# A decoder layer with routed experts: two ticks of attention scores joined into one round

## The chip, the core and the metric

The kernel runs on one core of one Trainium2 chip. The metric is the device time of one execution in microseconds. A run takes the whole layer: self-attention, cross-attention and a feed-forward part with 64 routed experts and a shared expert, all in fp32, for 32 sequences of 256 tokens and width 256.

## The reference

Cut to what matters here (16 heads, head width 16, T = 256 tokens, S = 120 context tokens):

```python
# self-attention, per sequence
q, k, v = heads(x @ qkv_w + qkv_b);  q, k = rotary(q), rotary(k)
x = layernorm(x + (softmax(q @ k.T * 16**-0.5) @ v) @ out_w + out_b)
# differential cross-attention: two half-heads of width 8
q1, q2 = halves(x @ qw.T + qb);  k1, k2 = halves(ctx @ kw.T + kb);  v = ctx @ vw.T + vb
a = softmax(q1 @ k1.T * 8**-0.5) - lam * softmax(q2 @ k2.T * 8**-0.5)
x = layernorm(x + ((a @ v) * (1 - LAMBDA_INIT)) @ out_proj.T + b)
# feed-forward: 6 of 64 experts per token, at most 96 rows per expert, and a shared expert
scores = sigmoid(x @ router.T); top 6; xs[slot] = x[token]
y = gelu(xs @ w1) @ w2;  out[token] += weight * y
x = layernorm(out + gelu(x @ sw1.T) @ sw2.T)
```

The routing goes over all 8192 tokens in order; a token that finds an expert's 96 rows taken gets nothing from it.

## The kernel before, in words

One stage makes both attentions and the routing for all 32 sequences ("batches" in the code); a second stage runs the experts in pairs, adds the shared expert's result and normalises. The change is in the first stage.

**Order.** Every engine is wrapped by `InOrder` (lines 166 to 192). It ties each instruction to the one before it on the same engine, so that each engine works in exactly the order in which the program writes the calls. All these calls are recorded with the wrapper's line 175; groups in the profile are therefore told apart by their tiles and not by their lines. Semaphores between engines come from the tiles: a buffer is written again when its last reader is done.

**Ticks.** `class Batch` writes its steps into the dictionary `plan`, keyed by tick and part. For each tick the loop at line 1015 runs "pre", then the score products, then their readers, then "av", "mm" and "post". "pre" mostly empties the PSUM banks that the tick before has filled; "mm" holds TensorE's other pieces: projections, transposes, the routing's products. A batch's self part starts at `start` and its cross part at `cross`. In the middle of the stage a new batch starts each 16 ticks, with its cross part 72 ticks after its self part. The first five self parts and the last four cross parts stand 8 ticks apart.

**Scores.** The softmax needs each row's maximum. So the scores are made twice. `maxima(k)` makes the scores of two heads with queries on the partitions, and VectorE reduces them (`pad_mx<-sc`). `turn_max` transposes the maxima, ScalarE copies them (`mT`), and GpSimd adds them into the queries' spare rows (`add_max`, `qT<-qT,mT`). Ten ticks after the maxima `weights(k)` makes the scores again, with keys on the partitions, and ScalarE takes the exponential (`pt<-sc`). A head uses 32 rows of the array. A tick has two heads' maxima on two strips of 32 rows and two heads' weights on the other two, so that four matmuls run side by side:

```python
for n in range(2):
    for mms, _ in pairs:
        for dst, lhsT, rhs in mms[2 * n : 2 * n + 2]:
            pe.matmul(dst, lhsT=lhsT, rhs=rhs, start=True, stop=True)
for _, read in pairs:
    read()
```

Each of these matmuls is two in the profile, as every fp32 matmul is; a tick's scores are 16 records. In the profile `sc<-qT,kT` are the weights and `sc<-kT,qT` the maxima.

**PSUM.** Of the eight banks, the pool `scp` has four, as two tiles of two banks (`sc`), and the pool `trp` four single banks (`tr`, `av`). A tick's two score tiles take both of `scp`; all other pieces share `trp`.

**Other pieces.** `values` and `xvalues` multiply the exponentials by the values (`av<-pt,pad_v`, 32-column strips); `back` and `xback` transpose the results, `weigh` and `xweigh` divide by the softmax's sums. `project_qk` and `rotate` make queries and keys, with the rotation on GpSimd (VectorE for the first batch). `heads` transposes them into `kT` and `qT`. `residual_1`, `residual_2`, `stats` and `normalise` close each attention; the routing follows (`router`, `route`, `places`, `keys`, `slots_of`). `dispatch` then scatters token rows into `slots` by indirect DMAs from GpSimd, twelve for a batch. The shared expert (`shared`) is a generator. Its pieces (tile `h` and others) are drawn one at a time near the stage's end and in the second stage.

Of the kernel before, what the change touches and what calls it, by code (L numbers as in the profile page):

```python
# [19 lines left out]
P = 128  # L20
# [17 lines left out]
def tile_decoder_layer(  # L38
# [74 lines left out]
    w_s1 = weights(sw1T, "w_s1")  # L113
    w_s2 = weights(sw2T, "w_s2")
# [81 lines left out]
    scp = ctx.enter_context(tc.tile_pool(name="scp", bufs=2, space=PSUM))  # L196
    trp = ctx.enter_context(tc.tile_pool(name="trp", bufs=4, space=PSUM))

    def bank():
        return trp.tile([P, 512], F32, tag="tr", name="tr")  # L200
# [4 lines left out]
    ys, whole = {}, set()  # L205

    def shared(ypool):
# [23 lines left out]
        before = None  # L231
        loaded = {k: load(k) for k in range(3)}
        gTs = {}
        for k in range(NBLK + 1):
            for f2 in range(2):
# [4 lines left out]
                if before:  # L240
                    before()
                hp = scp.tile([P, 2, 512], F32, tag="sc", name="h")
# [11 lines left out]
                before = lambda hp=hp, gT=gT: gelu(hp, gT)  # L254
                yield
            for q2 in range(NQ // 2):
                if k == 0:
                    continue
                if before:
                    before()  # L260
                ps = bank().rearrange("p (q d) -> p q d", q=2)
                for q in range(2):
                    for f in range(SF // P):
                        pe.matmul(
                            ps[:, q, :],
                            lhsT=gTs[k - 1, f // 2][
                                :, f % 2, (2 * q2 + q) * P : (2 * q2 + q + 1) * P
                            ],
                            rhs=w_s2[:, f, :],
                            start=(f == 0),  # L270
                            stop=(f == SF // P - 1),
                        )
                before = lambda k=k, q2=q2, ps=ps: keep(k - 1, q2, ps)
                yield
        before()
# [6 lines left out]
    with ExitStack() as one:  # L282
# [5 lines left out]
        small = one.enter_context(tc.tile_pool(name="small", bufs=2))  # L288
        hs = HD // 2
        TICKS = 16  # L290
# [24 lines left out]
        pad_mx = padded([P, NI, 4, PW], "pad_mx", 2)  # L315
# [11 lines left out]
        pad_xv = padded([P, H, PW], "pad_xv", 4, [lambda t: t[:, :, c0]])  # L327
# [51 lines left out]
        plan[-13, "pre"] = [(load_late, ())]  # L379
        for n in range(NE * CAP // (6 * P)):  # L380
            plan[40 + n, "pre"] = [(clear, (n,))]
        plan[5, "mm"] = [(fold, ())]
# [5 lines left out]
        class Batch:  # L388
            taken = None

            def __init__(self, b):
# [9 lines left out]
                turn = B - AHEAD  # L401
                blocks = (
# [3 lines left out]
                self.start, self.cross = (TICKS // 2 * n for n in blocks)  # L406
                self.m1, self.e1, self.m2, self.e2 = (
                    t + k for t in (self.start, self.cross) for k in (0, 10)
                )
                for begin, steps in ((self.start, self.steps()), (self.cross, self.steps_x())):  # L410
                    for tick, part, f, *args in steps:
                        plan.setdefault((begin + tick, part), []).append((f, args))

            def steps(self):


                return [
                    (-15 - (self.start if self.start <= TICKS else 0), "pre", self.load),
                    (-13, "mm", self.project_qk, 0),
                    (-12, "pre", self.rotate, 0),  # L420
                    (-11, "mm", self.project_qk, 1),
                    (-10, "pre", self.rotate, 1),
                    (7, "mm", self.project_v),
                    (8, "pre", self.put_v),
                    (-4, "mm", self.heads, "kT", 0, lambda i: self.qk[:, i, 1]),
                    (-4, "mm", self.heads, "kT", 1, lambda i: self.qk[:, i, 1]),
                    (-3, "pre", self.heads_moved, "kT", 0),
                    (-3, "pre", self.heads_moved, "kT", 1),
                    (-3, "mm", self.heads, "qT", 0, lambda i: self.qk[:, i, 0]),
                    (-2, "pre", self.heads_moved, "qT", 0),  # L430
                    (8, "pre", self.bias_x),
                    (0, "mm", self.heads, "qT", 1, lambda i: self.qk[:, i, 0]),
                    (1, "pre", self.heads_moved, "qT", 1),
                    (8, "mm", self.turn_max, 0),
                    (9, "pre", self.add_max, "qT"),
                    (14, "av", self.values, 0),
                    (14, "av", self.values, 1),
                    (15, "pre", self.values_moved, 0),
                    (18, "av", self.values, 2),
                    (18, "av", self.values, 3),  # L440
                    (19, "pre", self.values_moved, 1),
                    (20, "mm", self.back, 0),
                    (20, "mm", self.back, 1),
                    (21, "pre", self.weigh, 0),
                    (21, "pre", self.weigh, 1),
                    (24, "mm", self.transpose, "aT", lambda: self.at),
                    (25, "pre", self.moved, "aT"),
                    (25, "mm", self.project, "aT", "o", w_out),
                    (26, "pre", self.residual_1),
                    (26, "post", self.stats, 1),  # L450
                    (27, "post", self.normalise, 1),
                    (4 if self.start > TICKS else -14 - self.start, "pre", self.load_x),
                ]

            def steps_x(self):

                out = [
                    (-11, "mm", self.transpose, "x1T", lambda: self.x1),
                    (-9, "pre", self.moved, "x1T"),
                    (-9, "mm", self.project, "x1T", "q", w_xin[:, :, :D]),  # L460
                    (-8, "pre", self.put_q),
                    (2, "post", self.bias_x1),
                    (-8, "mm", self.heads, "yT", 0, lambda i: self.xq[:, i]),
                    (-6, "pre", self.heads_moved, "yT", 0),
                    (-4, "mm", self.heads, "yT", 1, lambda i: self.xq[:, i]),
                    (-3, "pre", self.heads_moved, "yT", 1),
                    (-20, "pre", self.cond_load),
                    (-13, "mm", self.cond_project),
                    (-12, "pre", self.put_kv),
                    (-9, "mm", self.keys_transpose, 0),  # L470
                    (-8, "pre", self.keys_moved, 0),
                    (-7, "mm", self.keys_transpose, 1),
                    (-6, "pre", self.keys_moved, 1),
                    (8, "mm", self.turn_max, 1),
                    (9, "pre", self.add_max, "yT"),
                    (14, "av", self.xvalues, 0),
                    (14, "av", self.xvalues, 1),
                    (15, "pre", self.xvalues_moved, 0),
                    (15, "pre", self.xvalues_moved, 1),
                    (18, "av", self.xvalues, 2),  # L480
                    (18, "av", self.xvalues, 3),
                    (19, "pre", self.xvalues_moved, 2),
                    (19, "pre", self.xvalues_moved, 3),
                    (20, "mm", self.xback, 0),
                    (21, "pre", self.xweigh, 0),
                    (21, "mm", self.xback, 1),
                    (22, "post", self.xweigh, 1),
                    (24, "mm", self.transpose, "bT", lambda: self.at),
                    (25, "pre", self.moved, "bT"),
                    (25, "mm", self.project, "bT", "o", w_xout),  # L490
                    (26, "pre", self.residual_2),
                    (26, "post", self.stats, 2),
                    (27, "post", self.normalise, 2),
                    (28, "mm", self.transpose, "x2T", lambda: self.xpt),
                    (29, "pre", self.moved, "x2T"),
                    (29, "pre", self.store),
                    (32, "mm", self.router),
                    (33, "pre", self.sigmoid),
                    (33, "post", self.route, 0),
                    (35, "post", self.route, 1),  # L500
                    (37, "post", self.route, 2),
                    (39, "post", self.route, 3),
                    (39, "post", self.route, 4),
                    (41, "mm", self.places),
                    (42, "pre", self.keys),
                    (42, "post", self.slots_of),
                ]
                ticks = iter(
                    (43, 43, 45, 47, 50, 51, 51, 52, 52, 53, 55, 55)
# [817 lines left out]
```

## Time and profile before

| | |
|---|---|
| median of 20 runs | 1962.12 us (1951.41 to 1969.15) |
| the profiled execution | 1960.52 us, span 1958.8 us, mean granted TensorE clock 0.982 |
| TensorE busy | 1874.9 us |
| VectorE busy | 1264.1 us |
| ScalarE busy | 1023.3 us |
| GpSimd busy | 1161.8 us |
| last score product | 1587 us after the span's start |
| last scatter of a token row | 1668 us |

The span is the time from the first to the last instruction that the profile records. Busy times of different engines lie beside each other. A matmul's end is modelled, so the start-to-start distances of matmuls say more than their durations.

### The profile page before, as it was taken

To read this page: it belongs to the slowest core of one execution; us is meant where nothing else is said; L and a number is where in the kernel's file an instruction comes from. 1 tells how busy PE (TensorE), PEld (TensorE's weight loads), DVE (VectorE), ACT (ScalarE), POOL (GpSimd) and SP (SyncE) were. 2 spreads that over 40 slices of the span, in tenths; PEclk is the share of its full clock that TensorE was granted. 3 is DMA by queue.
4 is the path that set the end of the run, shared out by engine and by line. 5 is a ranking of instruction groups with operands and counts; after the bars stand their busy time and mean duration, and the time that the engine had idled before them with its cause. 6 is when DMAs were issued, how large, how long until landed. Compare 5 with 4: busy or idle time off the path is not lost.

```text
span 1958.8 us, 43359 instructions
## 1 busy us (share of the span) xinstructions
PE 1874.9 (96%) x17800; PEld 1273.9 (65%) x17800; DVE 1264.1 (65%) x2812; ACT 1023.3 (52%) x1479; POOL 1161.8 (59%) x1155
## 2 busy tenths in 40 slices
PE   7999999999999999999999999999999879898985
PEld 4566666666666666666666666666666656576654
DVE  5456677777777777777777777777767752332175
ACT  1455555555555555555555555555555542321256
POOL 6433456666666666666666666666644567344665
PEclk9999999999999999999999999999999989898998
DMA  4053112111111111111111111111100123786486
GB/s 125 10 129 80 31 48 68 47 43 38 35 37 34 33 35 34 36 34 35 33 31 32 32 32 32 33 32 32 29 24 18 34 77 114 190 230 166 58 316 223
DMA packets 109542, 132.07 MB, mean 67 GB/s; under 512 B 33020, under 2 KB 94677, under 8 KB 109345
## 3 DMA queue, kind: packets, MB, share of 16 engines
q1 hardware_dynamic: 78832, 106.83, 17.6%
q0 software_dynamic: 25600, 13.02, 4.0%
q10 hardware_dynamic: 4912, 9.46, 1.3%
q8 instruction: 140, 2.29, 0.5%
q14 instruction: 58, 0.47, 0.1%
HBM read 74.62 MB, written 111.04 MB: 95 GB/s over the span
## 4 chain that ended last, share of the span: by engine, by line
PE 86%; DMA 6%; DVE 2%; issue 2%; POOL 2%; ACT 2%; ACTq 0%; POOLq 0%; DVEq 0%; SPq 0%
PE tr L175 43%; PE sc L175 28%; PE av L175 12%; DMA acc<-ye,idx 4%; PE h L175 3%; POOL slots L175 1%; DVE pad_mx L175 1%; ACT pt L175 1%; ACT four L175 1%; DMA slots<-xpt,slot 1%; DVE ye L175 0%; DMA xT<-in_xT 0%; DVE xpt L175 0%; DVE st L175 0%; ACT gT L175 0%
## 5 line engine op out<-in xcount | busy, mean ns | idle before, releaser
L175 DVE TENSOR_REDUCE pad_mx<-sc 128x4 f32<-128x1024 f32 (+1 forms) x512 | 609.0, 1190 | 358.7 <-PE sc L175 354.4
L175 ACT ACTIVATE pt<-sc 128x1024 f32<-128x1024 f32 (+1 forms) x512 | 525.0, 1026 | 403.2 <-PE sc L175 401.8
L175 PE MATMUL sc<-qT,kT 32*128 32x256 f32 (+1 forms) x4096 | 578.5, 401 | 8.3 <-ACT pt L175 8.2
L175 PE MATMUL sc<-kT,qT 32*128 32x256 f32 (+1 forms) x4096 | 568.0, 395 | 1.5 <-DVE pad_mx L175 1.5
L175 POOL DMA_INDIRECT slots<-xpt,slot x384 | 390.1, 1016 | 96.0 <-issue 91.4
L175 PEld LDWEIGHTS sc<-qT,kT 32*128 32x128 f32 (+1 forms) x4096 | 343.2, 181 | 131.0 <-issue 63.7
L175 PEld LDWEIGHTS sc<-kT,qT 32*128 32x128 f32 x4096 | 350.6, 185 | 72.4 <-issue 20.9
L175 POOL TENSOR_TENSOR qT<-qT,mT 128x512 f32<-128x512 f32 x128 | 159.6, 1267 | 157.9 <-ACT mT L175 157.9
L175 PE MATMUL tr<-w_qkv,xT 128*128 128x512 f32 (+1 forms) x512 | 194.3, 514 | 8.6 <-DMA xT<-in_xT 8.6
L175 POOL DMA_INDIRECT acc<-ye,idx x64 | 90.5, 1414 | 102.4 <-DVE ye L175 34.3
L175 ACT COPY ot<-av 128x512 f32<-128x512 f32 x192 | 112.6, 586 | 59.6 <-PE av L175 59.3
L175 PEld LDWEIGHTS tr<-w_qkv,xT 128*128 128x128 f32 x512 | 91.1, 192 | 76.6 <-issue 62.4
L175 PE MATMUL h<-x2T,w_s 128*128 128x512 f32 x256 | 123.4, 632 | 16.8 <-ACT gT L175 16.8
L175 POOL TENSOR_SCALAR rs<-mv 128x2 f32<-128x2 f32 x64 | 14.2, 221 | 201.6 <-DVE mv L175 201.5
L175 POOL TENSOR_TENSOR at<-parts 128x256 f32<-128x256 f32 x64 | 46.6, 728 | 141.0 <-DVE parts L175 140.9
L175 PE MATMUL av<-pt,pad_xv 120*32 120x256 f32 x2048 | 124.0, 382 | 0.7 <-ACT ot L175 0.7
L175 PE MATMUL av<-pt,pad_v 128*32 128x256 f32 x2048 | 123.8, 382 | 0.0
L175 PE MATMUL tr<-w_s,gT 128*128 128x256 f32 x512 | 115.9, 384 | 2.3 <-DVE ye L175 2.3
L175 ACT COPY kT<-tr 128x512 f32<-128x512 f32 (+1 forms) x128 | 70.2, 574 | 90.9 <-PE tr L175 90.9
L175 PEld LDWEIGHTS tr<-w_s,gT 128*128 128x128 f32 x512 | 98.0, 192 | 20.6 <-issue 3.8
L175 POOL TENSOR_TENSOR rc<-qkb,cosr 128x512 f32<-128x512 f32 x62 | 80.0, 1290 | 45.3 <-DVE qkb L175 37.3
L175 POOL TENSOR_TENSOR pad_qk<-rc,qkb 128x256 f32<-128x256 f32 x124 | 101.9, 843 | 4.9
(146 smaller groups left out, 2852.5 us busy)
## 6 DMA issues: line engine op xcount, KB each, us to landing
four<-in_w SPq DMA_DIRECT2D x32, 512.0 KB, 4.1
four<-acc SPq DMA_DIRECT2D x32, 512.0 KB, 6.0
xT<-in_xT SPq DMA_DIRECT2D x32, 256.0 KB, 3.4
xt<-in_x SPq DMA_DIRECT2D x32, 256.0 KB, 3.7
x2T_d<-T SPq DMA_DIRECT2D x32, 256.0 KB, 2.4
acc<-xpt SPq DMA_DIRECT2D x32, 256.0 KB, 2.6
acc<-zero SPq DMA_DIRECT2D x32, 256.0 KB
x2T<-x2T_d SPq DMA_DIRECT2D x16, 512.0 KB, 5.5
```

The costliest lines, as they stand in the source:

```text
L175: ins = f(*args, **kwargs)
```

## The change

Two ticks become one round. A round first writes both ticks' score products, four tiles of two banks, which is all of PSUM; then come the four readers, then the other pieces. The pool of the first stage is a ring of four tiles of two banks (`Ring`), from which score tiles and pieces are taken in turn: a piece takes half a tile, and a tile is handed out again when its last reader is done. In the second stage two pools stand apart as before (`Apart`). The weights' tile comes ahead of the maxima's. The table of steps is written anew in rounds; each step has a rank by which the steps of one round and part are sorted, and "av" is merged into "mm". The last batches' cross parts (`tail`) have offsets of their own.

The maxima tile `pad_mx` exists twice for each attention, by the batch's parity. `rotate` is split into `bias_qk` on VectorE, which reads the bank, and the rotation. Buffers: `xT` 3 to 4, `pt` 6 to 8, `xpt` 4 to 3, `pad_xv` 4 to 3. The shared expert's weights `w_s1` and `w_s2` are loaded when its pool opens, 15 rounds after the last batch's self start, and not at the start of the kernel. The arithmetic is unchanged.

```diff
-    scp = ctx.enter_context(tc.tile_pool(name="scp", bufs=2, space=PSUM))
-    trp = ctx.enter_context(tc.tile_pool(name="trp", bufs=4, space=PSUM))
+    class Ring:
+        def __init__(self, stack):
+            self.pool = stack.enter_context(tc.tile_pool(name="ring", bufs=4, space=PSUM))
+            self.half = None
+        def two(self):
+            self.half = None
+            return self.pool.tile([P, 2, 512], F32, tag="two", name="two")
+        def bank(self):
+            if self.half is None:
+                self.half = self.pool.tile([P, 2, 512], F32, tag="two", name="two")
+                return self.half[:, 0, :]
+            t, self.half = self.half, None
+            return t[:, 1, :]
...
-                self.start, self.cross = (TICKS // 2 * n for n in blocks)
+                self.start, self.cross = (4 * n for n in blocks)
...
+                    (-12 - self.start if first else -11, "pre", 0, self.load),
+                    (-10, "mm", 1, self.project_qk, 0),
+                    (-9, "pre", 1, self.bias_qk, 0),
+                    (-9, "post", 3, self.rotate, 0),
+                    (-9, "mm", 0, self.project_qk, 1),
+                    (-8, "pre", 1, self.bias_qk, 1),
+                    (-8, "post", 3, self.rotate, 1),
+                    (-2, "mm", 2, self.heads, "kT", 0, k),
+                    (-2, "mm", 2, self.heads, "qT", 0, q),
+                    (-2, "mm", 2, self.heads, "kT", 1, k),
+                    (-2, "mm", 2, self.heads, "qT", 1, q),
...
+                    (1, "mm", 2, self.project_v),
+                    (4, "mm", 0, self.turn_max, 0),
+                    (4, "post", 0, self.add_max, "qT"),
+                    (8, "mm", 1, self.values, 0),
...
+                    (9, "mm", 0, self.back, 0),
+                    (10, "pre", 0, self.weigh, 0),
+                    (10, "mm", 0, self.transpose, "aT", lambda: self.at),
+                    (11, "mm", 0, self.project, "aT", "o", w_out),
+                    (12, "pre", 0, self.residual_1),
+                    (13, "post", 1, self.stats, 1),
+                    (14, "post", 2, self.normalise, 1),
...
+                    (at(-7, -4), "mm", 2, self.cond_project),
+                    (at(-6, -3), "pre", 2, self.put_kv),
+                    (-5, "mm", 1, self.transpose, "x1T", lambda: self.x1),
+                    (-2, "mm", 1, self.project, "x1T", "q", w_xin[:, :, :D]),
+                    (-2, "mm", 3, self.keys_transpose, 0),
+                    (-1, "pre", 1, self.put_q),
+                    (-1, "mm", 3, self.heads, "yT", 0, lambda i: self.xq[:, i]),
+                    (0, "pre", 2, self.heads_moved, "yT", 0),
+                    (4, "mm", 0, self.turn_max, 1),
+                    (8, "mm", 1, self.xvalues, 0),
...
+                    (9, "mm", 0, self.xback, 0),
+                    (10, "pre", 0, self.xweigh, 0),
+                    (10, "mm", 0, self.xback, 1),
+                    (11, "pre", 0, self.xweigh, 1),
+                    (11, "mm", 2, self.transpose, "bT", lambda: self.at),
+                    (at(13, 12), "mm", 1, self.project, "bT", "o", w_xout),
+                    (at(14, 13), "pre", 1, self.residual_2),
+                    (at(14, 13), "post", 0, self.stats, 2),
+                    (at(15, 14), "pre", 3, self.normalise, 2),
+                    (at(15, 14), "mm", 1, self.transpose, "x2T", lambda: self.xpt),
+                    (at(17, 15), "mm", 1, self.router),
+                    (at(18, 16), "pre", 3, self.route, 0),
+                    (at(19, 16), "post", 1, self.route, 1),
+                    (at(21, 17), "post", 1, self.route, 3),
+                    (at(22, 17), "mm", 2, self.places),
+                    (at(24, 18), "post", 1, self.slots_of),
...
+                rounds = iter(
+                    (19, 19, 19, 20, 20, 20, 21, 21, 21, 22, 22, 22)
+                    if tail
+                    else (25, 25, 26, 29, 29, 29, 29, 30, 31, 31, 31, 31)
                 )
...
-                sc = scp.tile([P, 2, 512], F32, tag="sc", name="sc")
+                sc = psum[-1].two()
+                mx = pad_mx[cross][self.b % 2]
...
+        def run(n, part):
+            for _, f, args in sorted(plan.pop((n, part), ()), key=lambda step: step[0]):
                 f(*args)
+        def score_products(k):
+            pairs = []
+            for kind, behind in ((Batch.weights, 10), (Batch.maxima, 0)):
+                for bt in batches:
+                    if any(0 <= k - 2 * t - behind < 8 for t in (bt.start, bt.cross)):
+                        pairs.append(kind(bt, k))
             for n in range(2):
                 for mms, _ in pairs:
                     for dst, lhsT, rhs in mms[2 * n : 2 * n + 2]:
                         pe.matmul(dst, lhsT=lhsT, rhs=rhs, start=True, stop=True)
-            for _, read in pairs:
+            return [read for _, read in pairs]
+        for n in range(min(plan)[0], max(plan)[0] + 1):
+            if n == batches[-1].start + 15:
+                early_end.close()
+                ffns.append(ctx.enter_context(tc.tile_pool(name="ffn", bufs=2, side="right")))
+                next(pieces)
+            run(n, "pre")
+            for read in score_products(2 * n) + score_products(2 * n + 1):
                 read()
-            run(tick, "av")
-            run(tick, "mm")
-            if tick - batches[-1].cross in (20, 24, 27, 31, 34, 37, 39):
+            settle()
+            run(n, "mm")
+            if n - batches[-1].cross in (10, 12, 13, 14, 15, 16, 18):
                 next(pieces)
-            run(tick, "post")
+            run(n, "post")
```

## The prediction

> **What bounds the kernel now.** First the page's busy times and its chain of waits by engine.
>
> ```profile
> PE 1874.9 (96%) x17800; PEld 1273.9 (65%) x17800; DVE 1264.1 (65%) x2812; ACT 1023.3 (52%) x1479; POOL 1161.8 (59%) x1155
> ...
> PE 86%; DMA 6%; DVE 2%; issue 2%; POOL 2%; ACT 2%; ACTq 0%; POOLq 0%; DVEq 0%; SPq 0%
> ```
>
> TensorE is the bound. Next the busy times by stage (columns: PE, PEld, DVE, ACT, POOL, granted clock, DMA share, GB/s).
>
> ```profile
> 800.00:1000.00 200.00, 200.00 (x2133) 135.47 (x2123) 147.13 (x318) 114.33 (x165) 129.83 (x133) 1.00 0.12 34
> 1500.00:1550.00 50.00, 45.56 (x515) 31.20 (x512) 37.32 (x84) 29.18 (x43) 24.94 (x28) 1.00 0.06 18
> 1587.00:1667.00 80.00, 65.62 (x272) 42.62 (x268) 24.95 (x104) 24.24 (x24) 56.09 (x60) 0.91 0.28 89
> ```
>
> In the middle TensorE never idles: a batch takes 48.4 us (distance of one instruction to the same one of the next batch, 23 times running), 16 ticks of 3.02. Anything taken off TensorE there is won in full, unless it begins to wait. The timeline of TensorE shows what a tick is made of.
>
> ```profile
> 803.80 0.48 PE L175 MATMUL sc<-qT,kT 32*120 32x256 f32 x2
> 803.81 0.48 PE L175 MATMUL sc<-kT,qT 32*128 32x256 f32 x2
> 804.11 0.38 PE L175 MATMUL sc<-qT,kT 32*120 32x256 f32 x2
> ...
> 804.33 0.38 PE L175 MATMUL sc<-qT,kT 32*120 32x256 f32 x2
> ...
> 804.55 0.38 PE L175 MATMUL sc<-qT,kT 32*120 32x256 f32 x2
> ...
> 804.88 0.66 PE L175 MATMUL tr<-ident,xpt 128*128 128x128 f32 x4
> ...
> 806.77 0.48 PE L175 MATMUL sc<-qT,kT 32*120 32x256 f32 x2
> ```
>
> Four waves of four matmuls on 32-row strips start 0.31, 0.22 and 0.22 us apart, and the pieces follow 0.33 after the last. So a stretch of scores takes 1.08 where four waves at 0.216 are 0.86, and the last piece before it is followed 0.09 late (a 512-column matmul by 0.523 us in place of 0.429). Each stretch costs 0.097 + 0.115 + 0.093 = 0.305 us at its edges, and the first interval of the pieces behind it is 0.05 (transposes) to 0.10 (matmuls) longer.
>
> The readers of the even tick that starts at 803.80 (timelines of ScalarE and VectorE):
>
> ```profile
> 805.03 1.03 ACT L175 ACTIVATE pt<-sc 120x1024 f32<-120x1024 f32 x1 [2.02 <-PE sc L175]
> ```
> ```profile
> 805.03 1.23 DVE L175 TENSOR_REDUCE pad_mx<-sc 128x4 f32<-128x1024 f32 x1 [0.33 <-PE sc L175]
> ```
>
> Both begin 1.23 us after the first score. At present nobody on TensorE waits for them, since the pieces have four banks of their own.
>
> **What the change saves.** Eight stretches per batch in place of sixteen: 8 x 0.305 = 2.44. First intervals: 1.17 over the 16 ticks (seven pieces begin with matmuls at 0.104, five with transposes at 0.055, four with av at 0.043); afterwards 0.81 over eight rounds (two at 0.104, six at 0.055, and turn_max before values adds two switches to column strips of 0.13 each). Together 2.8: TensorE's work falls from 48.4 to 45.6 us per batch.
>
> One page speaks for the switch and against its use: the Trainium skill, "TensorEngine Tiling (Array Packing)", says under Tiling Modes that a change of tiling mode drains TensorE, and under PSUM Bottleneck that after tiling the copying out of PSUM may become the limit. By another, "TensorE: Matmul & The Clock Gate", section Step-by-step, the drain of one matmul overlaps the fill of the next; by that rule alone a switch is free, the saving is nil, and the sum below would end 70 us later. The measured edges decide for a saving.
>
> **The wait that it adds.** The four score tiles fill all eight banks, and the ring hands them out in turn: the first piece of a round always gets the slot of the round's own first tile (weights of tick 2n), so it waits for that tile's exponential. First score at 0; exponential from 1.235 to 2.261 (1.026 mean); TensorE starts 0.053 after a release by ScalarE (0.052 to 0.053 in 12 of 18 cases, 0.144 in the others): 2.315. Without the wait it would start at 0.097 + 8 x 0.216 + 0.115 = 1.94. So 0.37 us idle in each round, 8 x 0.37 = 3.0 per batch, against the 2.8 saved. Queued behind this piece is everything on TensorE.
>
> Later pieces find their banks read: the reduction ends at 2.45, the second exponential (start 0.921 behind the first) at 3.18, the second reduction at 3.6; the pieces that get them start after 2.7, 4.1 and 5.4 in most rounds.
>
> **Where a round waits once more.** By round modulo 8 (self start = 0), TensorE's pieces with edges: 0 turn_max, values 3.96; 1 back, o, v 4.48; 2 transpose, q, places, keys 3.56; 3 o, x2T, yT 3.23; 4 turn_max, xvalues 3.96; 5 xback, router, cond 3.64; 6 xback, qk, four heads 4.48; 7 qk, two transposes 2.79. Sum 30.1, plus 8 x 2.315 gives 48.6. I then laid the readers of each round in order, with start-to-start times of the trace (VectorE: reduction 1.08 or 1.14, stats 1.08, xweigh 1.69, weigh 1.27, qk bias 0.67, normalise 0.65; ScalarE: copy 0.47 to 0.59):
> - Round 4's cross maxima need yT, whose transposes stand near the end of round 3; behind the copy of x2T its copy ends 0.30 after the round's start: +0.34.
> - Round 7's second tile takes the slot that bias_qk reads. VectorE's queue from the end of round 5's reductions: stats 1.08, xweigh 1.69, put_kv 0.40, route 1.19, two reductions 2.15, normalise 0.65, xweigh 1.69, bias 0.69: 9.5 us, and 9.35 until round 7: +0.22 with the release.
> - Rounds 0 to 3, 5 and 6 have 0.1 us or more in hand (least: the copies of the last piece, 0.8 against 0.957, when the second half starts).
>
> Period 48.6 + 0.56 = 49.1, or +0.7. Unknown ends: 48.1 if the exponential starts at 1.17 as in odd ticks and nothing else waits (-0.3); 50.5 if releases take 0.144 (+0.7) and VectorE's queue is 0.7 longer. I take 49.1, worked from the even rows. Rounds 32 to 236 are 25.5 periods: +18 us (-8 to +53).
>
> **Before and after that.** Ticks 10 to 42 (self batches only, four rounds each) took 25.2 us per batch; the same sum gives 14.4 of pieces, 9.3 of stretches and 0.6 of waits, 24.3, so -4. Rounds 0 to 4 have two tiles each and free slots, and add_max no longer stands behind a second rotation on GpSimd (the trace stalls there: 16.4 us for ticks 8 to 12 against 12): -3, and +1 up to round 32. Cross batches alone (rounds 240 to 256, one each four rounds, 24.2 us now): after a round with 7.6 us of pieces comes one with 1.5, in which VectorE still has stats, routes and xweigh (5.9 us from its start), and the next round's third tile waits for xweigh: TensorE stands 2 us there and 2 at its M slot; 28.7 us, four times +4.5: +18, and +1 to the last scores.
>
> Then GpSimd's scatters decide (chain of waits, end of the stage):
>
> ```profile
> 1658.88 0.97 POOL slots L175
> 1660.16 0.97 POOL slots L175
> 1661.43 0.97 POOL slots L175
> ```
>
> One starts each 1.27 us. At the last scores (1587) 55 are left, the last at 1668. The new table issues them three per round from offset 19, so about 40 are left: 15 x 1.27 = 19, taken as -20. The third xpt buffer, with four before, costs nothing while a batch's scatters end three rounds before its successor's residual; else it adds to this chain (0 to 15).
>
> The rest: w_s1 and w_s2 (1 MB) leave the crowded start (DMA 0.79 busy in the first 20 us) and load 15 rounds before they are needed; SP's loads keep their places ahead of the stores and land in 3 to 4 us, a round ahead; mx per parity, pt 8 and the split of bias and rotation only loosen; the expert stage keeps its pools.
>
> Sum: +18 - 6 + 19 - 20 = +11. The profiled execution took 1960.5 (span 1958.8), the median is 1962.1: 1973.
>
> A page against the change: "TensorE: Matmul & The Clock Gate", psum-queue depth-cycling, tells of a kernel whose clock fell because TensorE idled briefly between groups as it cycled through banks. Here 1500 to 1550 has TensorE 91% busy with waits up to 1.1 us, and the clock stays 1.00; were it to fall to 0.95 all through, an estimate by that page would add some 60 us.
>
> **Rivals.** Below 0.2% (4 us) a measurement of this kernel can't tell a change.
> 1. Faster, 1930: the exponential starts at 1.17, VectorE is ahead in round 7 and in the cross-only stage. -8 - 6 + 1 - 20 = -33. It decides when TensorE's mean idle per round is under 0.3. For it: VectorE is 74% busy; against: even ticks start at 1.23 throughout.
> 2. VectorE becomes the bound, 2020: 0.05 us more for each of the 31 instructions of the 9.5 us queue is +1.5 per batch, +38; and the scatters save nothing, +20. It decides once that queue passes 9.4 us, which it does already by my sum.
> 3. The fill is paid again between the halves, because weights and maxima exchange strips there: 0.21 saved in place of 0.305, +0.8 per batch, 1993. No stretch of 32 without a wait is in the trace.
>
> **Numbers.** My forecast 0.38 (own range 1955 to 1995; same 0.10, slower 0.28), rival 1 0.28, rival 2 0.22, rival 3 0.12. Faster 0.28, same 0.10, slower 0.62. The range leaves out the far ends of rivals 1 and 2: 1932 to 2022.
>
> **What would show it.** Right: stretches of 32 scores lasting 1.94; TensorE idle before each round's first piece, 0.37 us, released by the exponential; a period near 49.1 with longer waits in rounds 4 and 7; last scatter sooner behind the last scores than 81 us. Wrong: a first piece that doesn't wait, a second half that starts late, or a clock under 1.00.

## The result, and the profile after

The changed kernel takes 2085.6 us (median of nine runs, 2077.5 to 2088.5) against 1963.5: 1.062 times the time before, 95% interval 1.060 to 1.063. Slower was forecast, but 1973 us, and the upper end of the range was 2022. The profiled execution has a span of 2081.7 us, 122.9 more than the one before.

First the page of the changed kernel: busy times, and the chain that ended last.

```profile
PE 1927.4 (93%) x17800; PEld 1363.7 (66%) x17800; DVE 1315.6 (63%) x2811; ACT 994.2 (48%) x1479; POOL 1146.6 (55%) x1156
...
PE 53%; DVE 13%; issue 12%; POOL 10%; ACT 6%; DMA 5%; ACTq 0%; DVEq 0%; POOLq 0%
```

TensorE held 86% of the chain before and holds 53% now. No other engine takes its place: VectorE, GpSimd and ScalarE share the rest, the look of a chain that goes from engine to engine. The stages (columns as in the prediction):

```profile
800.00:1000.00 200.00, 191.17 (x1985) 135.11 (x1988) 140.47 (x289) 102.93 (x154) 115.66 (x120) 1.00 0.12 34
1600.00:1650.00 50.00, 47.36 (x480) 33.21 (x480) 32.86 (x76) 25.53 (x40) 22.68 (x24) 0.93 0.21 70
1720.00:1783.00 63.00, 54.66 (x252) 34.84 (x251) 22.86 (x93) 24.66 (x26) 46.81 (x51) 0.94 0.35 110
```

In the middle (first line) TensorE still looks 96% busy, but it made 1985 matmuls in 200 us where it made 2133 before: part of its waits lies inside what counts as busy. The clock is 1.00. A batch now takes 52.5 us. The 122.9 us by stage, from one of the 512 maxima reductions to the same one in both traces: up to number 64, -5.3; to number 464, +104.1; to the last exponential, +33.8; from there to the last scatter, -17.7; behind it, +8.0. The second row above is from the rounds with cross batches alone, the third from the scatters behind them; their clock is 0.93 and 0.94.

A round as forecast, and the worst one (TensorE's timeline):

```profile
835.03 0.48 PE L173 MATMUL two<-qT,kT 32*128 32x256 f32 x2
...
836.82 0.38 PE L173 MATMUL two<-kT,qT 32*128 32x256 f32 x2
837.28 0.44 PE L173 MATMUL two<-ident,pad_mx 128*128 128x128 f32 x2
```
```profile
828.64 0.70 PE L173 MATMUL two<-qT,kT 32*128 32x256 f32 x4 [0.31 <-DVE parts L173]
829.76 0.47 PE L173 MATMUL two<-kT,qT 32*128 32x240 f32 x2 [0.42 <-ACT kT L173]
...
832.24 1.98 PE L173 MATMUL two<-w_qkv,xT 128*128 128x512 f32 x4
```

Round 0 (835.03): the first piece follows 2.25 us after the first score, released by the exponential; forecast 2.315. Round 7 (828.64): 3.60. Its scores of the second tile wait 0.42 for a copy on ScalarE named kT. That copy moves one of the *heads*, an engine away from VectorE's queue, and yet (timelines of VectorE and ScalarE):

```profile
828.41 0.68 DVE L173 TENSOR_TENSOR qkb<-two,b_qk 128x512 f32<-128x512 f32 x1
```
```profile
829.12 0.58 ACT L173 COPY kT<-two 128x512 f32<-128x512 f32 x1 [4.65 <-DVE qkb L173]
```

The 4.65 us are ScalarE's idle time ahead of the copy. The four transposes that it copies had ended at 827.02; the 2.1 us after that it stood behind bias_qk, of which it needs nothing. They have only the ring's tile in common: qk lies in one half, kT in the other. The list of waits (idle time of the waiting engine in total, times, longest) shows that this is no single case:

```profile
ACT kT L173 <- DVE qkb L173: 131.6, 28, 9.8
...
ACT pad_v L173 <- DVE xpt L173: 115.7, 26, 4.8
...
ACT T L173 <- DVE x L173: 63.6, 26, 2.5
```

Each comes 26 or 28 times, about once per batch: kT behind qk, v behind the cross o, x2T behind the self o. In round 5's tile of router and cond it goes back and forth:

```profile
821.27 0.49 DVE L173 TENSOR_TENSOR pad_xk<-two,b_xqk 120x128 f32<-120x128 f32 x2 [0.22 <-ACT two L173]
822.25 0.29 DVE L173 TENSOR_SCALAR sg<-two 128x128 f32<-128x128 f32 x1 [0.49 <-ACT pad_xv L173]
```
```profile
820.98 0.26 ACT L173 ACTIVATE two<-two 128x128 f32<-128x128 f32 x1 [2.92 <-PE two L173]
821.85 0.37 ACT L173 COPY pad_xv<-two 120x256 f32<-120x256 f32 x1 [0.61 <-DVE pad_xk L173]
```

The exponential of the router's sigmoid, put_kv on VectorE, put_kv on ScalarE, route: each waits for the one before on the other engine, because the program orders readers by tile. The queue of a tile's readers is a chain over two engines, and the tile is free at its end.

### The profile page after: what moved, and what is told of

It reads as the page before. It is cut to its first block, busy times and chain, and to the rows that moved or that the text cites. A ratio compares the mean times of both kernels' runs of the same rounds, so it can differ in the third digit from the quotient of the medians.

```text
span 2081.7 us, 43571 instructions
## 1 busy us (share of the span) xinstructions
PE 1927.4 (93%) x17800; PEld 1363.7 (66%) x17800; DVE 1315.6 (63%) x2811; ACT 994.2 (48%) x1479; POOL 1146.6 (55%) x1156
## 3 DMA queue, kind: packets, MB, share of 16 engines
q8 instruction: 141, 2.31, 0.5%
## 4 chain that ended last, share of the span: by engine, by line
PE 53%; DVE 13%; issue 12%; POOL 10%; ACT 6%; DMA 5%; ACTq 0%; DVEq 0%; POOLq 0%
PE two L173 48%; PE one L173 5%; DMA acc<-ye,idx 5%; DVE pad_mx L173 4%; ACT pt L173 3%; DVE x L173 3%; POOL pad_qk L173 2%; POOL qT L173 2%; POOL qkb L173 2%; POOL rc L173 2%; DVE sg L173 2%; DVE parts L173 1%; DVE rd L173 1%; POOL at L173 1%; ACT qT L173 1%
## 5 line engine op out<-in xcount | busy, mean ns | idle before, releaser
L173 DVE TENSOR_REDUCE pad_mx<-two 128x4 f32<-128x1024 f32 (+1 forms) x512 | 592.9, 1185 | 338.6 <-PE two L173 337.9
L173 PE MATMUL two<-qT,kT 32*128 32x256 f32 (+1 forms) x4096 | 566.5, 400 | 21.5 <-DVE parts L173 13.7
L173 PE MATMUL two<-kT,qT 32*128 32x256 f32 (+1 forms) x4096 | 529.5, 393 | 41.9 <-ACT qT L173 11.3
L173 ACT ACTIVATE pt<-two 128x1024 f32<-128x1024 f32 (+1 forms) x512 | 506.7, 1027 | 109.6 <-PE two L173 109.0
L173 PEld LDWEIGHTS two<-qT,kT 32*128 32x128 f32 (+1 forms) x4096 | 342.8, 182 | 129.7 <-issue 71.5
L173 PEld LDWEIGHTS two<-kT,qT 32*128 32x128 f32 x4096 | 347.7, 185 | 110.5 <-ACT qT L173 29.9
L173 PE MATMUL two<-w_qkv,xT 128*128 128x512 f32 (+1 forms) x512 | 190.9, 507 | 13.2 <-DMA xT<-in_xT 8.6
L173 POOL DMA_INDIRECT acc<-ye,idx x64 | 90.5, 1413 | 110.2 <-DVE ye L173 52.5
L173 PE MATMUL two<-x2T,w_s 128*128 128x512 f32 x256 | 119.3, 615 | 9.7 <-ACT gT L173 9.7
L173 PE MATMUL two<-pt,pad_xv 120*32 120x256 f32 x2048 | 117.1, 381 | 0.0
L173 PE MATMUL two<-pt,pad_v 128*32 128x256 f32 x2048 | 117.1, 381 | 0.0
```

Source lines behind the costliest of these rows:

```text
L173: ins = f(*args, **kwargs)
```

## The experiments

Theory A: the halves of one ring tile are read by two engines, which wait for each other. Theory B: VectorE's queue is longer than summed. Some runs came from a second chip, on which the kernel before takes 1981 to 1986 us; so ratios go by the runs of before beside each, and periods are compared on one chip only.

**Tiles with one reader (e1).** `bank` is given the reading engine, and two pieces share a tile only if it is the same (cut to the test).

```
-            if self.half is None:
-                self.half = self.pool.tile([P, 2, 512], ...)
+            if self.half is None or self.half[0] != by:
+                self.half = by, self.pool.tile([P, 2, 512], ...)
```

> Two pieces share a tile of the ring only if the same engine reads both; otherwise a piece takes a tile alone. The number of instructions stays. Theory A (two engines that read the halves of one tile wait for each other, so ScalarE's copies stand behind VectorE's queue): the period falls from 52.5 us by 1.5 to 3 us, rounds 3 and 4 lose most of their late waves, and no copy on ScalarE waits for VectorE's qkb, xpt or x any more; time 2005 to 2047 us. Theory B (VectorE's queue alone is longer than my sum): the same queue holds the same slots, the period changes by under 0.5 us; 2072 to 2090 us.

Second chip: 2078.8 us, 1.047 (1.043 to 1.052). Period 51.5; the unedited kernel there has 54.0 (below). The waits of kT, pad_v and T for VectorE are gone from the list. A by its size, -2.5, though the time in us is that of a slower chip. Round 4's first piece comes 2.69 us after its first score, as in e8 below; round 3's still comes after 3.12. One wait grew: TensorE idles 1.01 us ahead of round 7, for VectorE (0.33 unedited). The edit also moves pieces to other slots of the ring, which no run separates from the order of the readers; for the order speak the waits that are gone.

**A lighter VectorE (e3).** Left out: a reciprocal of the router and the self half's normalisation.

```
-                    dve.reciprocal(sg, sg)
     def normalise(self, n):
+        if n == 1: return
```

> The changed kernel with 2.2 us less per batch in VectorE's queue between the reductions of round 5 and bias_qk of round 7: the reciprocal of the router's first step (0.95 us) and the first normalisation (two instructions, 1.24 us) are left out. Theory B: round 7's wait goes and the rounds behind it follow, the period falls by 1.5 to 2.5 us; 2020 to 2047 us. Theory A alone: only the wait of round 7 shrinks, by 0.6 to 1.2 us, those of rounds 2, 3, 4 and 6 stay; 2055 to 2071 us.

1.062 (1.058 to 1.066), period 53.1: 0.9 less than unedited. Round 7's first piece comes 3.23 us after its first score in place of 3.60, and the 0.33 before the round is gone; rounds 2, 3, 4 and 6 keep their waits. That is what A alone expected.

**Both (e4).**

> Both edits together: tiles shared by one reader only, and the 2.2 us left out of VectorE's queue. If the causes are separate, the two gains add: period 48.5 to 49.5 us, 1975 to 2005 us. If they are one (a copy is late only since VectorE is late), the gain is no larger than the larger of the two alone.

1.033 (1.028 to 1.037), period 50.6: 3.4 less, the sum of 2.5 and 0.9. The gains add, so the causes are separate, and A is the larger; the wait before round 7 is down to 0.18. The absolute figures expected were those of the first chip.

**The unedited kernels on the second chip (c_after, c_before).**

> The changed kernel once more, unedited, as the measure for the runs beside it. In the three experiments on its ring two of TensorE's signals came 0.4 to 2.2 us late once per batch, in round 2, which the first trace of the changed kernel does not show. If that belongs to the chip, it is here too and the period is near 53 us; if it belongs to the edits, the period is 52.5 us again. Ratio to the kernel before 1.055 to 1.065 in both cases.

2142.9 us, 1.078 (1.074 to 1.081), above the ratio expected; period 54.0, and the late signals are there without any edit, so they come with this chip and not with the edits. Round 2 in VectorE's, TensorE's and GpSimd's timelines:

```profile
866.68 1.23 DVE L173 TENSOR_REDUCE pad_mx<-two 128x4 f32<-128x1024 f32 x1 [0.79 <-PE two L173]
869.62 1.23 DVE L173 TENSOR_REDUCE pad_mx<-two 128x4 f32<-128x1024 f32 x1 [1.71 <-remote]
```
```profile
867.10 0.60 PE L173 MATMUL two<-kT,qT 32*128 32x256 f32 x4
867.63 0.66 PE L173 MATMUL two<-ident,at 128*128 128x128 f32 x4
```
```profile
866.50 0.97 POOL L173 DMA_INDIRECT slots<-xpt,slot  x1 [0.30 <-issue]
867.77 0.97 POOL L173 DMA_INDIRECT slots<-xpt,slot  x1 [0.30 <-issue]
```

The last scores start by 867.3 and end at 867.7, and TensorE goes on; the reduction that waits for them starts at 869.62. "remote" is a semaphore update to which the trace finds no instruction.

> The kernel before, unedited, for its profile on the same chip: period 48.4 us as in its first trace; if late signals belong to the chip, 48.8 to 49.2 us and some 15 us more in all.

1982.9 us, period 48.5, TensorE busy throughout. Neither figure as expected: signals are late here too (over 100 of 857 beside scatters, by over 0.3 us), but TensorE, with separate banks, does not wait for them in the middle (busy 200 of 200 us). The 22 us more lie mostly behind the middle (+16 in the cross-only stage).

**The ring alone undone (e2).** Scores in two tiles of two banks and pieces in four single banks, as before; a round's scores and pieces in two parts.

```
-            for read in score_products(2 * n) + score_products(2 * n + 1): read()
-            run(n, "mm")
+            for h in range(2):
+                for read in score_products(2 * n + h): read()
+                # half of the round's pieces
```

> The new step table, but scores and pieces have PSUM of their own as before the change (two score tiles of two banks, four single banks), one tick's scores at a stretch and half of a round's pieces behind each. Theories A and B both put the loss on the shared ring: TensorE is busy without idling again, the period is 48 to 49 us, the scatters still end sooner behind the last scores; 1935 to 1965 us. Rival C (the new places of the steps make the waits, whatever PSUM they use): the period stays above 50.5 us; over 2020 us.

2301.6 us, 1.160 (1.155 to 1.164), period 58.5 to 60.6: A and B missed, and the figures lie where C put them. TensorE's timeline in round 6:

```profile
812.31 0.38 PE L173 MATMUL two<-qT,kT 32*128 32x256 f32 x2
814.29 0.66 PE L173 MATMUL tr<-ident,pad_qk 128*128 128x128 f32 x4 [1.60 <-ACT kT L173]
815.68 1.46 PE L173 MATMUL tr<-ident,pad_qk 128*128 128x128 f32 x8 [0.73 <-ACT qT L173]
```

Seven banks of pieces in one round find four, and the copies that free them stand behind the next scores' exponentials. These waits come from the edit itself, so it neither convicts nor acquits the table of rival C: it shows that table and ring belong together, and not what the table costs. What speaks against C is e8 below, which keeps the table and reaches the forecast's period.

**Theory A's size without late signals (e7, e8).** These two runs came from a chip like the first (1962.5 us for the kernel before).

> The changed kernel without the scatters of 30 of its 32 batches (their rows stay empty; the expert stage does the same work on them). On this chip TensorE's signals were up to 2.8 us late, and nearly all late ones lay inside a stretch of scatters on GpSimd. If the scatters delay the signals, none is late now, the period falls from 54.0 us to the 52.5 us of the first trace or a little under, and round 3's third wave starts near 0.4 again. If not, the period stays at 53.5 us or more. (The time as a whole is of no use: the stage behind the last scores is shorter.)

Period 51.9, no late signal. As on this chip none is late with the scatters either, that question isn't answered; but the scatters themselves cost the changed kernel 0.6 us per batch (52.5 with them): GpSimd is 38% busy in place of 58%, and the 0.31 us wait at round 7's start is gone. From 800 to 1000 us, this run and then the next:

```profile
800.00:1000.00 200.00, 192.41 (x1996) 136.43 (x1991) 140.67 (x290) 104.16 (x156) 75.13 (x78) 1.00 0.10 30
800.00:1000.00 200.00, 195.71 (x2109) 145.19 (x2106) 148.05 (x306) 111.22 (x164) 79.94 (x84) 1.00 0.10 30
```

> The kernel whose tiles are shared by one reader only, without the same scatters, to size theory A with no late signals in it. Theory A: 1.5 to 3 us under the period of the changed kernel without scatters, so 49.5 to 51 us. If the gain of the first experiment came from where the late signals fell, under 0.5 us remains.

Period 49.1: 2.8 under the run above, near the upper end of what theory A expected. No ScalarE copy of a piece waits for VectorE now but pad_xv, whose bank has two readers by nature. The table gives where the 2.8 lie (median us from a round's first score to its first piece; the last column is of a later experiment):

| round | forecast | changed kernel | no scatters | and one reader | e9 |
|---|---|---|---|---|---|
| 0, 1 | 2.32 each | 2.26, 2.25 | 2.26, 2.25 | 2.30, 2.31 | 1.94, 1.94 |
| 2 | 2.32 | 2.60 | 2.54 | 2.31 | 1.94 |
| 3 | 2.32 | 2.88 | 2.88 | 2.25 | 2.46 |
| 4 | 2.66 | 2.98 | 2.98 | 2.69 | 1.89 |
| 5 | 2.32 | 2.32 | 2.32 | 2.32 | 1.90 |
| 6 | 2.32 | 2.88 | 2.88 | 2.26 | 2.12 |
| 7 | 2.54 | 3.60 | 3.47 | 2.35 | 1.89 |
| sum | 19.1 | 21.8 | 21.6 | 18.8 | 16.1 |

**VectorE's steps spread (e5).** The first experiment's tiles, and in the table (shortened; the last batches keep the old places):

```
-   (13, "post", 1, self.stats, 1), (14, "post", 2, self.normalise, 1),
+   (16, "pre", 5, self.stats, 1), (16, "post", 6, self.normalise, 1),
-   route 3, 4 at (21, "post")
+   route 3, 4 at (24, "pre")
    heads before qk, yT before o, places beside q
```

> Tiles shared by one reader only, and VectorE's steps spread: the statistics and normalisation of the self half, and the router's last two steps, go to rounds in which VectorE idled; heads stand before qk, yT before o, and the places share a tile with q. Nothing is left out. Theory A with a crowded queue as second cause: the waits of rounds 2, 3, 6 and 7 go, what stays is the first piece's wait for the exponential in all eight rounds (8 x 0.37 us) and 0.34 in round 4: period 49 to 50 us, ratio to the kernel before 1.00 to 1.02. If the waits only move to other rounds, the period stays above 51 us, ratio over 1.04.

Second chip: 2045.3 us, 1.029 (1.024 to 1.034), period 51.3: the period lies where the waits only move (above 51), the ratio between the two cases. From first score to first piece rounds 0, 1, 2, 5, 6 and 7 have 2.26 to 2.32, the wait for the exponential alone (a later piece of round 2 waits 0.45 more). Most of what is left stands in round 4, whose second half waits 1.34 us for residual_1: VectorE gets the signal of o's last product 2.7 us late, in a stretch of scatters.

**The first piece's wait (e6).** On top: the first weights tile of a round as two tiles of one bank.

```
+   banks = [psum[-1].one() for _ in range(2)]
-   act.activation(pt[:n], sc[:n], AF.Exp, scale=scale)
+   for j in range(2):
+       act.activation(pt[:n, j], banks[j][:n], AF.Exp, scale=scale)
```

> The same, and the first score tile of a round is two tiles of one bank, each with an exponential of its own (512 columns in place of 1024), so the first piece waits only for the first half of that exponential; two pieces of a round get these single banks. If the first piece's wait is worth what the prediction gave it (0.37 us in each of eight rounds), the period falls by 2.5 to 3 us against the same table without it, to 46 to 47.5 us, and the kernel is faster than before: ratio 0.96 to 0.985. If TensorE's first piece is held by something else at that point, the period falls by under 1 us.

Same chip: 2048.9 us, 1.032 (1.029 to 1.035), period 50.8, in every third batch 52.1. The first piece now starts 1.89 to 1.94 us after the first score in five of the eight rounds, 0.32 to 0.42 earlier than in e5: the wait was of the size forecast. The time is the same, because two other waits grew: round 4's, to 1.8 in about half of the batches (late signals again), and a new one of 2.0 in round 1, for a reduction that stands behind these (VectorE's and GpSimd's timelines):

```profile
810.10 2.52 DVE L173 TENSOR_TENSOR count<-count,sel 128x64 f32<-128x64 f32 x2
812.55 2.41 DVE L173 TENSOR_SCALAR x<-x,mv,rstd 128x256 f32<-128x256 f32 x2
```
```profile
812.62 1.28 POOL L173 TENSOR_TENSOR qkb<-qkb,sinr 128x512 f32<-128x512 f32 x1
```

The normalisation's two instructions take 1.51 and 0.99 us beside GpSimd's multiplications, 0.41 each in the trace of before. But in e5 they were slow in this place too (1.37 and 1.36), and round 1 did not wait. New here is that GpSimd's additions start 1.5 us sooner in the round, and that the router's two counts, now beside them, take 1.30 and 1.20 in place of 0.22. The reduction is late by both together.

The 52.1 of every third batch has another cause, the granted clock. Behind round 1's wait it is 0.50 for 3.41 us, from 764.31 on:

```profile
764.00:768.00 4.00, 3.94 (x10) 3.14 (x11) 2.64 (x7) 0.00 (x0) 3.09 (x4) 0.57 0.03 7
```

That round takes 10.36 us, and 8.67 in the batches whose clock stays 1.00.

**The normalisation elsewhere (e9).** In the table (shortened; the last batches keep the old place):

```
-   (16, "post", 6, self.normalise, 1)
+   (20, "pre", 6, self.normalise, 1)
```

> The table with single banks at the round's start, and the self half's normalisation moved from round 0, where it ran beside GpSimd's additions and took 2.41 us in place of 0.74, to the start of round 4, where VectorE stood idle beside scatters. Theory D (VectorE's two-operand and scalar steps wait while GpSimd adds): it takes 0.8 us or less there, the wait of 2.0 us before round 1's product o goes, and the period falls by 1.5 to 2 us, from 50.8 to 49 us. If the step is slow wherever it stands, the wait moves with it and the period stays.

1915.1 us on a chip like the first, **0.976 (0.972 to 0.980) of the kernel before**: faster than both, and than the kernel before by 2.0 to 2.8%. Period 46.6. The normalisation takes 0.406 us an instruction again and round 1 has no wait, though the counts are as slow as in e6: 2.25 of the fall from 50.8 lie there. Round 4's wait is gone too, 1.84 us; as this chip has no late signals, that part is put down to the chip. How much the table (e5) and the single banks (e6) give by themselves on this chip wasn't run.

```profile
827.94 0.73 DVE L173 TENSOR_SCALAR x<-x,mv,rstd 128x256 f32<-128x256 f32 x2
```
```profile
800.00:1000.00 200.00, 199.75 (x2227) 145.02 (x2224) 162.70 (x330) 116.93 (x206) 135.49 (x140) 1.00 0.12 33
```

TensorE makes 2227 matmuls in 200 us, against 2133 before the change and 1985 after it.

**The scatters spread (e10).**

```
-   (25, 25, 26, 29, 29, 29, 29, 30, 31, 31, 31, 31)
+   (25, 25, 26, 26, 27, 27, 28, 28, 29, 30, 30, 31)
```

> The same with the twelve scatters of a batch spread over rounds 1 to 7 in place of four each in rounds 5 and 7. If stretches of scatters hold back TensorE's signals, the waits of 1.3 to 1.8 us in round 4 shrink and the period is 0.5 to 1.5 us shorter than without the spread, 47.5 to 48.5 us, which would be faster than the kernel before (ratio 0.97 to 0.99). If the number of scatters counts and not their spacing, it is the same within 0.3 us.

1920.5 us, 0.977 (0.973 to 0.982), period 47.0, 0.4 longer and all of it in round 1: no gain, and neither case as expected. This chip has no late signals, so whether spreading helps where they occur isn't told.

## Why the prediction was right or wrong

- **The failed step** is "Rounds 0 to 3, 5 and 6 have 0.1 us or more in hand". Rounds 0, 1 and 5 did; rounds 2, 3 and 6 waited 0.29 to 0.57. The readers of each round were laid in order for each engine by itself; that readers of one tile follow each other across engines was left out. The sizes of rounds 4 and 7 failed with it: +0.66 and +1.29 (and 0.31 before round 7), where +0.34 and +0.22 were forecast. With one reader to a tile, round 4 has +0.37 and round 7 +0.03.
- **Its size.** The period was 52.5 against 49.1 forecast: 3.4 us, of which 2.8 is theory A and 0.6 the scatters beside it; without both it is 49.1. Over the 25 periods between reductions 64 and 464, that is +104 in place of +18. The forecast let the scatters cost nothing in the middle, without a reason: that is the 0.6. The trace of before had the hint, from the one bank whose two readers, on two engines, share no data:

```profile
ACT pad_xv L175 <- DVE pad_xk L175: 8.7, 5, 2.5
```

It cost nothing then and was passed over.
- **What the change saves** held: a stretch of 32 scores with nothing in its way lets the pieces start after 1.94 us (e9, three rounds).
- **The wait that it adds** held: 2.25 to 2.32 where nothing else waits, forecast 2.315, and where the first bank is freed sooner (e6), 0.32 to 0.42 us of it go.
- **Before and after.** Ramp -5.3 (-6 forecast), scatters -17.7 (-20; 45 were left at the last scores, 40 forecast): held as sums, whose terms weren't looked at singly. Rounds with cross batches alone: +33.8 (+19 forecast), too small by 15. The best version still has +26 there. The +8 behind the last scatter were not settled; that stage's length also changed between kernels with the same code for it (283 to 304 us).
- **The clock.** The prediction counted on 1.00, by the kernel before in 1500 to 1550, and named a clock under 1.00 as a sign against it. In the middle it held. In the rounds with cross batches alone it didn't (from reduction 464 to the last exponential, before and after):

```profile
1421.70:1587.40 165.70, 155.77 (x1707) 107.39 (x1706) 118.08 (x279) 97.36 (x141) 80.27 (x85) 1.00 0.12 37
1520.50:1720.00 199.50, 177.33 (x1721) 126.86 (x1714) 130.82 (x304) 94.81 (x141) 98.47 (x104) 0.92 0.12 38
```

The missing 0.08 of 199.5 us is 16 us, an estimate of the most that this can have cost, and about the 15 that the forecast lacks. No run changes the clock alone, so it isn't shown; without scatters (e7) this stage has 0.98 and takes 178.9 us.
- **Rivals.** 1 (faster) failed: it needed under 0.3 us of idle time per round, and the first pieces alone come 0.78 behind the 1.94 of a stretch without a wait (mean 2.72). 2 (VectorE's queue is the bound) has a part: 2.2 us taken from the queue gave 0.9 per batch, at and in round 7, where it was expected, and the normalisation, 0.65 in that queue's sum, took 1.24 (825.52); the larger part of the waits was ScalarE's, behind VectorE through the shared tiles. The time stated for rival 2 doesn't add up: 1973 + 38 + 20 is 2031 and not 2020. 3 (the fill is paid again between the halves) failed: where nothing waits the second half follows at 0.20 to 0.24 us (e9, rounds 0 to 2), not at the 0.31 of a fresh stretch, and the 1.94 has no second fill in it.
- **The two rules.** By the Trainium skill, "TensorEngine Tiling (Array Packing)", section PSUM Bottleneck, copying out may become the limit once TensorE is packed; the changed kernel agrees (TensorE's chain share from 86% to 53%), and the limit was the order of the copies, not their rate: ScalarE is half idle. What "TensorE: Matmul & The Clock Gate", psum-queue depth-cycling, tells did not come true in the middle, where TensorE idled in every round and the clock stayed 1.00; the 0.92 of the last rounds is of its kind, and e6's 0.50 followed one longer wait. The 0.95 and 60 us that the prediction worked with are of its own choosing; the page gives neither.

## What to carry to other kernels

A PSUM tile with two halves was one object to what ordered this program: with two engines reading its halves, the slower queue held the faster engine and the tile. Pair pieces by the engine that reads them before summing queues, and read the list of waits for releases between instructions that share no data. When all banks are lent to one producer, ask which bank comes back first, and make that one small: two half-size exponentials took away the wait that the forecast had set against the whole saving.

## What was not expected of the hardware

- On the second chip TensorE's completion signals came late (after the modelled end of their matmul) beside GpSimd's scatters: of the unedited changed kernel's signals between 250 and 1400 us, 97 of 420 within a scatter or 1.5 us behind it were over 0.3 us late, by up to 2.3 us (2.8 in e6), and 21 of 686 elsewhere. On the first chip 0 of 400 and 22 of 738. Those elsewhere were at most 0.37 us late on both. In the round shown above the matmuls start within 0.02 us of the same place on both. Whether the scatters cause it was only argued from this: the run without them came from the other chip.
- A wait of 2.0 us was enough to halve TensorE's clock, but not always: in e6 every batch waits so long in round 1, and from 600 to 1250 us the clock is 0.50 for 3.41 us five times, 153.6 us apart, in one batch of three. In the 3.41 us ahead of the first three of these TensorE was busy for a share of 0.41 or 0.42.
- The normalisation's two instructions took 2.4 to 2.7 us together beside GpSimd's additions and multiplications (e6, e5), 0.406 each away from them; the router's counts took 1.30 and 1.20 in place of 0.22. The Trainium skill, "SBUF — State Buffer", section Who interferes with whom, has VectorE and GpSimd share one port pair under an exclusive lock; that fits, and the sum of the prediction had 0.65 for this step wherever it stood.
